# Layer norm averages in one matmul: sums folded to 64 partitions, and attention issued three steps sooner

## The chip, the core and the metric

One NeuronCore of a Trainium2 chip runs the kernel. The metric is the device time of one execution in microseconds; for the kernel before, three runs gave a median of 1599.13 us. TensorE is called PE here, VectorE DVE, ScalarE ACT, GpSimd POOL and SyncE SP, as in the profile.

## The reference

A block with layer norm ahead of each half, on x of shape (2, 4096, 256), in fp32:

```
def _layernorm(x, axis=-1, eps=1e-05):
    m = jnp.mean(x, axis=axis, keepdims=True)
    v = jnp.var(x, axis=axis, keepdims=True)
    return (x - m) / jnp.sqrt(v + eps)
...
x = x + attn(_layernorm(x))     # mixes of x and the token before; k, v, r; a scan over time (WKV); W_o
x = x + ffn(_layernorm(x))      # silu(w1 h) * (w2 h), gelu(h1 .), gelu(h2 .), w3; hidden width 1024
```

Each linear layer of the ffn has weights of -1, 0 and 1 and one scale per output. The attention part is an RWKV time mix: k, v and r are products of mixed inputs with 256 x 256 weights, the WKV recurrence runs along the 4096 tokens, and its result times sigmoid(r) goes through W_o.

## The kernel before

**Layout and tiles.** Features lie on partitions (256 features are two halves of 128), tokens along the free dimension. The tokens are cut into 16 tiles of 512. For each tile the work is: layer norm (`normalise`), attention (`attention`), a second layer norm at attention's end, and `ffn`.

**Precision.** An ffn operand is split into a rounded part hi and a remainder lo (`split`, L190: ACT copies to the rounded type, DVE subtracts), and each weight block is multiplied with both (`split_product`, L180, lines 185 and 186). A product for attention (`product`, L178) is in fp32 and takes two passes in the records, each about twice as long.

**Layer norm.** A mean over 256 features is a sum over partitions, made on PE with the constant matrix `mean_wr` (all entries 1/256), which also spreads the result over all partitions. `layernorm` (L201) adds the two halves into `both` (L206), and `average` (L195) splits that sum into hi and lo and runs two matmuls into one PSUM bank. The centred halves (L212) are squared on ACT (L217), added (L218), averaged in the same way, then root (L220, ACT), reciprocal (L222, DVE) and the multiplication (L224). Tiles 1 to 15 have two such norms each, so two means and two variances. Tile 0 has a function of its own (`first_layernorm`) that the change doesn't touch.

**Order.** The functions are generators. While `ffn(i)` runs, its loop also advances `attention(i+1)` and `normalise(i+2)`. `ffn` has 26 steps: 8 gated products (pa and pb), 8 products of the first hidden layer, 8 of the second (both called ph), and 2 outputs (po). This order of writing is only a start: the framework schedules instructions on each engine when the program is built, so that the built order departs from it, but later steps come later. [...] The loop in the kernel before is:

```
            if step >= NH:
                next(ahead, None)
            if step > 2 * NH - 2 and step % 2:
                next(further, None)
```

Here NH is 8, `ahead` is `attention(i + 1)` and `further` is `normalise(i + 2)`. The pieces of attention are: three mixes (mx, L313 and L314), then for each half h a group of products ps_k, ps_v, ps_r and three pieces of `wkv`, then the output products ps_o with the addition to x (L335), and the three pieces of the second norm, after which x2 is split (x2_hi, x2_lo).

**Buffers.** The products of the ffn rotate through 4 PSUM banks, those of attention through 3, and all averages share 1. Three x tiles rotate; the load of a new one (POOL's queue) waits for the output transfer of the tile that had the buffer. The blocks of h2 come through SP's queue. `compare` (L163) holds copies of weights against the originals, in the same loop[...]. A second program, `general_block`, follows under a condition that isn't met here.

Of the kernel before, what the change touches and what calls it, by code (L numbers as in the profile page):

```python
# [7 lines left out]
F32 = mybir.dt.float32  # L8
F32R = mybir.dt.float32r
AF = mybir.ActivationFunctionType  # L10
ALU = mybir.AluOpType

P = 128
B, T, D, HID = 2, 4096, 256, 1024
TS = 512
ND = D // P
NH = HID // P
# [21 lines left out]
@with_exitstack  # L39
def tile_rwkv_block(  # L40
    ctx: ExitStack,
    tc: tile.TileContext,
    x: bass.AP,
    vecs: bass.AP,
    w_attn: bass.AP,
    w1: bass.AP,
    w2: bass.AP,
    h1: bass.AP,
    h2: bass.AP,
    w3: bass.AP,  # L50
    out: bass.AP,
):
    nc = tc.nc
    flags = ctx.enter_context(tc.tile_pool(name="flags", bufs=1))
    with ExitStack() as inner:
        inexact = split_block(inner, tc, flags, x, vecs, w_attn, w1, w2, h1, h2, w3, out)
    count = nc.values_load(inexact, min_val=0, max_val=1)
    with tc.If(count > 0):
        with ExitStack() as inner:
            general_block(inner, tc, x, vecs, w_attn, w1, w2, h1, h2, w3, out)  # L60


def split_block(ctx, tc, flags, x, vecs, w_attn, w1, w2, h1, h2, w3, out):
# [3 lines left out]
    tensor, vector, scalar = nc.tensor, nc.vector, nc.scalar  # L67
# [4 lines left out]
    one = ctx.enter_context(tc.tile_pool(name="one", bufs=1))  # L72
# [5 lines left out]
    ps_sum = ctx.enter_context(tc.tile_pool(name="ps_sum", bufs=1, space=bass.MemoryType.PSUM))  # L78
# [46 lines left out]
    mean_wr = const.tile([P, P], F32R, name="mean_wr")  # L125
# [29 lines left out]
    pieces = []  # L155
    for sb, src in ((w1_sb, w1), (w2_sb, w2), (h1_sb, h1), (w3_sb, w3)):
        n = src.shape[1] * src.shape[2] // PIECE
        sb, src = (t.rearrange("p a b -> p (a b)") for t in (sb, src))
# [21 lines left out]
    def split_product(psum, weights, src):  # L180

        n = len(src)
        for c in range(n):
            hi, lo = src[c]
            tensor.matmul(psum, weights(c), hi, start=c == 0, stop=False)  # L185
            tensor.matmul(psum, weights(c), lo, start=False, stop=c == n - 1)  # L186

    marks = {}

    def split(hi, lo, full):  # L190

        marks["scalar"] = scalar.activation(hi, full, AF.Copy)  # L192
        marks["split"] = vector.tensor_tensor(lo, full, hi.bitcast(F32), ALU.subtract)  # L193

    def average(psum, both):  # L195

        pieces = one.tile([P, 2, TS], F32R, tag="sums", name="sums")
        split(pieces[:, 0, :], pieces[:, 1, :], both)
        split_product(psum, lambda c: mean_wr, [(pieces[:, 0, :], pieces[:, 1, :])])

    def layernorm(src, new_xc, tag, pause=False):  # L201


        both = one.tile([P, TS], F32, tag=tag, name="both")
        mean = ps_sum.tile([P, TS], F32, tag="ps", name="mean")
        vector.tensor_tensor(both, src[:, 0, :], src[:, 1, :], ALU.add)  # L206
        average(mean, both)
        if pause:
            yield
        xc = new_xc()  # L210
        for h in range(ND):
            vector.tensor_tensor(xc[:, h, :], src[:, h, :], mean, ALU.subtract)  # L212
        yield
        sq = wide.tile([P, ND, TS], F32, tag="wide", name="sq")
        var = ps_sum.tile([P, TS], F32, tag="ps", name="var")
        rstd = one.tile([P, TS], F32, tag=tag, name="rstd")
        scalar.activation(sq, xc, AF.Square)  # L217
        vector.tensor_tensor(sq[:, 0, :], sq[:, 0, :], sq[:, 1, :], ALU.add)  # L218
        average(var, sq[:, 0, :])
        scalar.activation(rstd, var, AF.Sqrt, bias=eps)  # L220
        yield
        vector.reciprocal(rstd, rstd)  # L222
        for h in range(ND):
            vector.tensor_tensor(xc[:, h, :], xc[:, h, :], rstd, ALU.mult)  # L224
        yield
# [58 lines left out]
    def normalise(i):  # L284

        x_sb = loaded.pop(i)
        if i + 1 < len(tiles):
            loaded[i + 1] = load_x(i + 1)
        xn = []

        def new_xn():

            xn.append(one.tile([P, ND, TS + 1], F32, tag="xn", name="xn"))
            if tiles[i][1] == 0:
                vector.memset(xn[0][:, :, 0:1], 0.0)
            else:
                vector.tensor_copy(xn[0][:, :, 0:1], prev)
            return xn[0][:, :, 1:]

        yield from layernorm(x_sb, new_xn, "rstd1", pause=i == 1)  # L300
        vector.tensor_copy(prev, xn[0][:, :, TS:])
        normal[i] = (x_sb, xn[0])

    def attention(i):

        first = tiles[i][1] == 0
        x_sb, xn = normal.pop(i)
        mixed = []
        for m in range(3):
            mx = wide.tile([P, ND, TS], F32, tag="wide", name="mx")  # L310
            for h in range(ND):
                j = m * ND + h
                vector.tensor_scalar(mx[:, h, :], xn[:, h, 0:TS], unmix[:, j : j + 1], None, ALU.mult)  # L313
                vector.scalar_tensor_tensor(  # L314
                    mx[:, h, :], xn[:, h, 1:], vec[:, j : j + 1], mx[:, h, :], ALU.mult, ALU.add
                )
            mixed.append(mx)
            yield

        y = wide.tile([P, ND, TS], F32, tag="wide", name="y")  # L320
        for h in range(ND):
            kvr = []
            for m, name in enumerate("kvr"):
                ps = ps_attn.tile([P, TS], F32, tag="pa", name="ps_" + name)
                product(
                    ps, lambda c: wa_sb[:, m, c, h * P : (h + 1) * P], [mixed[m][:, c, :] for c in range(ND)]
                )
                kvr.append(ps)
            yield
            yield from wkv(h, *kvr, y, first)  # L330

        for h in range(ND):
            ps = ps_attn.tile([P, TS], F32, tag="pa", name="ps_o")
            product(ps, lambda c: wa_sb[:, 3, c, h * P : (h + 1) * P], [y[:, c, :] for c in range(ND)])
            vector.tensor_tensor(x_sb[:, h, :], x_sb[:, h, :], ps, ALU.add)  # L335
        yield
        x2 = wide.tile([P, ND, TS], F32, tag="wide", name="x2")
        yield from layernorm(x_sb, lambda: x2, "rstd2")
        x2_hi = one.tile([P, ND, TS], F32R, tag="x2_hi", name="x2_hi")
        x2_lo = one.tile([P, ND, TS], F32R, tag="x2_lo", name="x2_lo")  # L340
        split(x2_hi, x2_lo, x2)
        got[i] = (x_sb, [(x2_hi[:, c, :], x2_lo[:, c, :]) for c in range(ND)])
# [186 lines left out]
    def run(steps):  # L529
        for _ in steps:  # L530
            pass
# [15 lines left out]
    for i in range(len(tiles)):  # L547
        ahead = attention(i + 1) if i + 1 < len(tiles) else iter(())
        further = normalise(i + 2) if i + 2 < len(tiles) else iter(())
        for step, _ in enumerate(ffn(i, *got.pop(i))):  # L550
            if i == 0 and step % 2:
                next(second, None)

            if step >= NH:
                next(ahead, None)
            if step > 2 * NH - 2 and step % 2:
                next(further, None)
        run(ahead)
        run(further)
# [287 lines left out]
```

## Time and profile before

| | us |
|---|---|
| three runs, median (lowest to highest) | 1599.13 (1598.64 to 1599.64) |
| the profiled execution, own time | 1599.32 |
| its span, first to last instruction | 1597.5 |
| matmuls of the averages, both parts: mean 18.9 + 12.6, variance 12.2 + 12.4 | 56.1 busy, 120 matmuls |
| ACT table loads with Gelu (L508), and with the root (L220) | 130.9 (102 loads), 38.5 (30 loads) |
| reciprocal of the norm, DVE (L222) | 100.4 (30, 3.35 each) |

The span is what the profile covers; the own time has 1.8 us more. In a group's row the numbers behind the bar are the busy time of all its instructions and the mean of one in ns, then the idle time of the engine just ahead of them and what ended it. Matmuls overlap in the records: a hidden-layer matmul lasts 0.39 us there, but the next starts 0.23 us later.

In the steady part a tile takes about 96.5 us (the output products ps_o of two tiles in a row start 96.45 us apart, at 710.23 and 806.67). The last PE instruction ends at 1588.3 us; what follows is the last output transfer and the check of the comparisons.

### The profile page before, as it was taken

The page shows a single profiled execution, that of the slowest core. Times are in us where ns is not written, and L with a number is a line of the kernel's source. Part 1 is how long each engine was busy: PE and PEld are TensorE (multiplying, and loading weights), DVE is VectorE, ACT ScalarE, POOL GpSimd, SP SyncE. Part 2 cuts the span into 40 slices and gives each one's busy share as a digit, 9 for nine tenths or more (in the row PEclk, how much of TensorE's full clock was granted, in tenths as well). Part 3 has the DMA queues.
Part 4 walks back from the last instruction along what each step waited for, and adds up shares of the span by engine and source line. Part 5 has one row for each costly group of instructions (what it writes and reads, how often), then busy time and mean ns, then how long its engine had stood idle before and what let it go on. Part 6 is the DMA issues. An engine that isn't in the chain of part 4 may idle for free.

```text
span 1597.5 us, 16645 instructions
## 1 busy us (share of the span) xinstructions
PE 1576.5 (99%) x6370; PEld 1198.3 (75%) x6370; DVE 1063.3 (67%) x1707; ACT 1005.7 (63%) x1337; POOL 58.0 (4%) x92
## 2 busy tenths in 40 slices
PE   8899999999999999999999999999999999999997
PEld 4677778777777777777777777777778777787786
DVE  5767577685766958668585676857668575675521
ACT  5566666756757567576666657567576666657542
POOL 2000000000000000000000000000000000000000
PEclk9899999999999999999999999999999999999999
DMA  9103122130311203112030221203112031211202
GB/s 357 38 0 109 37 80 73 33 119 14 106 54 53 93 14 119 40 56 96 20 119 27 80 72 46 93 14 106 40 53 86 7 105 40 67 60 33 93 8 74
DMA packets 36790, 109.17 MB, mean 68 GB/s; under 512 B 3680, under 2 KB 12384, under 8 KB 36192
## 3 DMA queue, kind: packets, MB, share of 16 engines
q1 hardware_dynamic: 19552, 68.71, 13.0%
q0 software_dynamic: 16736, 38.80, 7.9%
q8 instruction: 52, 0.85, 0.2%
q10 hardware_dynamic: 416, 0.52, 0.1%
q14 instruction: 34, 0.28, 0.1%
HBM read 99.64 MB, written 12.58 MB: 70 GB/s over the span
## 4 chain that ended last, share of the span: by engine, by line
PE 80%; issue 15%; DMA 1%; ACT 1%; DVE 1%; POOL 0%; SPq 0%; POOLq 0%; ACTq 0%
PE ph L185 24%; PE ph L186 24%; PE pa L185 3%; PE pb L185 3%; PE pa L186 3%; PE pb L186 3%; PE po L186 3%; PE po L185 3%; PE ps_r L178 3%; PE ps_k L178 3%; PE ps_v L178 3%; PE ps_o L178 3%; DMA wa_sb<-in_w_attn 1%; PE mean L185 0%; PE mean L186 0%
## 5 line engine op out<-in xcount | busy, mean ns | idle before, releaser
L185 PE MATMUL ph<-hi,h_sb 128*128 128x512 f32 x2048 | 812.3, 397 | 0.0
L186 PE MATMUL ph<-lo,h_sb 128*128 128x512 f32 x2048 | 799.9, 391 | 0.0
L185 PEld LDWEIGHTS ph<-hi,h_sb 128*128 128x128 f32 x2048 | 384.6, 188 | 89.7 <-issue 7.4
L186 PEld LDWEIGHTS ph<-lo,h_sb 128*128 128x128 f32 x2048 | 384.7, 188 | 87.2 <-issue 7.2
L511 DVE TENSOR_TENSOR lo<-full,hi 128x512 fp32r<-128x512 f32 x256 | 175.1, 684 | 314.8 <-ACT full L510 314.6
L508 ACT ACTIVATE hi<-ph,vec 128x512 fp32r<-128x512 f32 x256 | 176.0, 687 | 288.4 <-PE ph L186 287.0
L510 ACT ACTIVATE full<-ph,vec 128x512 f32<-128x512 f32 x256 | 174.4, 681 | 0.0
L508 ACT ACT_TABLE_LOAD x102 | 130.9, 1283 | 1.8
L492 ACT ACTIVATE gated<-pa,vec 128x512 f32<-128x512 f32 x128 | 86.9, 683 | 63.2 <-PE pa L186 60.2
L493 DVE SCALAR_TENSOR_TENSOR gated<-pb,vec,gated 128x512 f32<-128x512 f32 x128 | 95.3, 748 | 30.1 <-PE pb L186 21.6
L185 PE MATMUL pa<-x_hi,w_sb 128*128 128x512 f32 x256 | 103.9, 406 | 1.7 <-ACT gated L492 1.7
L186 PE MATMUL pa<-x_lo,w_sb 128*128 128x512 f32 x256 | 103.4, 404 | 0.0
L222 DVE RECIPROCAL rstd<-rstd 128x512 f32<-128x512 f32 x30 | 100.4, 3346 | 3.3 <-ACT rstd L220 3.2
L185 PE MATMUL pb<-x_hi,w_sb 128*128 128x512 f32 x256 | 102.0, 398 | 0.0
L186 PE MATMUL pb<-x_lo,w_sb 128*128 128x512 f32 x256 | 100.8, 394 | 0.0
L192 ACT ACTIVATE hi<-gated 128x512 fp32r<-128x512 f32 x128 | 80.3, 629 | 32.2 <-DVE gated L493 30.9
L186 PE MATMUL po<-lo,w_sb 128*128 128x512 f32 x256 | 98.1, 392 | 0.0
L185 PE MATMUL po<-hi,w_sb 128*128 128x512 f32 x256 | 97.9, 391 | 0.0
L193 DVE TENSOR_TENSOR lo<-gated,hi 128x512 fp32r<-128x512 f32 x128 | 87.6, 685 | 12.5 <-ACT hi L192 9.1
L314 DVE SCALAR_TENSOR_TENSOR mx<-xn,vec,mx 128x512 f32<-128x512 f32 x90 | 66.2, 745 | 0.4
L260 ACT ACTIVATE sc<-sc 128x512 f32<-128x512 f32 x32 | 20.3, 633 | 67.0 <-DVE sc L258 66.9
L185 PEld LDWEIGHTS pa<-x_hi,w_sb 128*128 128x128 f32 x256 | 48.5, 189 | 17.2 <-ACT gated L492 4.1
(140 smaller groups left out, 1774.9 us busy)
## 6 DMA issues: line engine op xcount, KB each, us to landing
h_sb<-h_hbm SPq DMA_DIRECT2D x128, 512.0 KB, 3.3
out<-x_sb POOLq DMA_DIRECT2D x16, 512.0 KB, 3.1
raw<-in_h POOLq DMA_DIRECT2D x32, 256.0 KB, 3.1
x_sb<-in_x POOLq DMA_DIRECT2D x14, 512.0 KB, 4.0
h_sb<-in_h POOLq DMA_DIRECT2D x1, 4096.0 KB, 20.2
h_hbm<-in_h POOLq DMA_DIRECT2D x8, 512.0 KB, 25.3
w_sb<-in_w POOLq DMA_DIRECT2D x3, 1024.0 KB, 10.4
raw<-in_w POOLq DMA_DIRECT2D x12, 256.0 KB, 2.8
```

Of the source, the lines that this page charges most:

```text
L178: tensor.matmul(psum, weights(c), src[c], start=c == 0, stop=c == n - 1)
L185: tensor.matmul(psum, weights(c), hi, start=c == 0, stop=False)
L186: tensor.matmul(psum, weights(c), lo, start=False, stop=c == n - 1)
L192: marks["scalar"] = scalar.activation(hi, full, AF.Copy)
L193: marks["split"] = vector.tensor_tensor(lo, full, hi.bitcast(F32), ALU.subtract)
L222: vector.reciprocal(rstd, rstd)
L314: vector.scalar_tensor_tensor(mx[:, h, :], xn[:, h, 1:], vec[:, j : j + 1], mx[:, h, :], ALU.mult, ALU.add)
L492: scalar.activation(full, pa, AF.Silu, scale=col(S1, f))
L493: vector.scalar_tensor_tensor(full, pb, col(S2, f), full, ALU.mult, ALU.mult)
L508: scalar.activation(hi, ps, AF.Gelu, scale=col(scales, f))
L510: scalar.activation(full, ps, AF.Gelu, scale=col(scales, f))
L511: vector.tensor_tensor(lo, full, hi.bitcast(F32), ALU.subtract)
```

## The change

`average` now takes the two addends, makes the sum itself, and folds it: the upper 64 partitions of the sum are copied by ACT to the lower 64, DVE adds the lower 64, and the result (64 partitions) is split so that hi lies on partitions 0 to 63 and lo on 64 to 127 of one tile. One matmul with the same constant matrix then sums both. The squares are no longer added in place but into the tile `both`. And the loop takes four pieces of attention at step 8, and pieces of the norm after next at steps 12, 14, 16 and 18 instead of 15, 17, 19 and 21.

```
-    def average(psum, both):
-
-        pieces = one.tile([P, 2, TS], F32R, tag="sums", name="sums")
-        split(pieces[:, 0, :], pieces[:, 1, :], both)
-        split_product(psum, lambda c: mean_wr, [(pieces[:, 0, :], pieces[:, 1, :])])
+    def average(a, b, tag, name):
+
+
+        both = one.tile([P, TS], F32, tag=tag, name="both")
+        vector.tensor_tensor(both, a, b, ALU.add)
+        folded = one.tile([P // 2, TS], F32, tag="folded", name="folded")
+        marks["scalar"] = scalar.activation(folded, both[P // 2 :, :], AF.Copy)
+        vector.tensor_tensor(folded, folded, both[: P // 2, :], ALU.add)
+        parts = one.tile([P, TS], F32R, tag="parts", name="parts")
+        split(parts[: P // 2, :], parts[P // 2 :, :], folded)
+        psum = ps_sum.tile([P, TS], F32, tag="ps", name=name)
+        tensor.matmul(psum, mean_wr, parts, start=True, stop=True)
+        return psum
...
-        both = one.tile([P, TS], F32, tag=tag, name="both")
-        mean = ps_sum.tile([P, TS], F32, tag="ps", name="mean")
-        vector.tensor_tensor(both, src[:, 0, :], src[:, 1, :], ALU.add)
-        average(mean, both)
+        mean = average(src[:, 0, :], src[:, 1, :], tag, "mean")
...
-        var = ps_sum.tile([P, TS], F32, tag="ps", name="var")
+        scalar.activation(sq, xc, AF.Square)
+        var = average(sq[:, 0, :], sq[:, 1, :], tag, "var")
         rstd = one.tile([P, TS], F32, tag=tag, name="rstd")
-        scalar.activation(sq, xc, AF.Square)
-        vector.tensor_tensor(sq[:, 0, :], sq[:, 0, :], sq[:, 1, :], ALU.add)
-        average(var, sq[:, 0, :])
...
-            if step >= NH:
+            for _ in range(0 if step < NH else 4 if step == NH else 1):
                 next(ahead, None)
-            if step > 2 * NH - 2 and step % 2:
+            if step > 2 * NH - 6 and step % 2 == 0:
                 next(further, None)
```

## The prediction

> **What bounds the kernel now.** I read the busy shares first, then the list of waits (PE's alone), the chain, and the timeline of one tile.
>
> ```profile
> PE 1576.5 (99%) x6370; PEld 1198.3 (75%) x6370; DVE 1063.3 (67%) x1707; ACT 1005.7 (63%) x1337; POOL 58.0 (4%) x92
> PE 80%; issue 15%; DMA 1%; ACT 1%; DVE 1%; POOL 0%; SPq 0%; POOLq 0%; ACTq 0%
> PE pa L185 <- ACT gated L492: 1.7, 2, 1.3
> ```
>
> PE is busy for the whole span, and the chain of work that ended last lies on it. The third line is the only wait of PE listed after the first tile's attention ends (some 57 us); the others add to under 11 us, all earlier. So the span is a count of matmuls times their spacing, and ACT and DVE (about a third idle) count only where PE would wait for them. In the stage table of one tile (the gated products, hidden layer 1, hidden layer 2, the output product) only the first presses on DVE, 13.46 of 15.40 us:
>
> ```profile
> 736.50:751.90 15.40, 15.40 (x66) 12.12 (x65) 13.46 (x22) 9.84 (x16) 1.43 (x2) 1.00 0.20 70
> 751.90:793.00 41.10, 41.10 (x162) 30.12 (x161) 22.27 (x42) 25.40 (x34) 1.10 (x2) 1.00 0.04 13
> 793.00:829.00 36.00, 36.00 (x152) 27.94 (x151) 27.98 (x41) 26.39 (x34) 1.51 (x2) 1.00 0.36 117
> ```
>
> (Columns: length; busy us and count of PE, weight loads, DVE, ACT, POOL; granted clock.) The clock is full throughout, so no gain can come from it.
>
> **What is removed.** PE's timeline around the mean of an attention output:
>
> ```profile
> 719.42 0.39 PE L185 MATMUL ph<-hi,h_sb 128*128 128x512 f32 x1
> 719.66 0.50 PE L185 MATMUL mean<-sums,mean_wr 128*128 128x512 f32 x1
> 720.00 0.39 PE L186 MATMUL ph<-lo,h_sb 128*128 128x512 f32 x1
> 720.22 0.39 PE L185 MATMUL ph<-hi,h_sb 128*128 128x512 f32 x1
> 720.45 0.44 PE L186 MATMUL mean<-sums,mean_wr 128*128 128x512 f32 x1
> 720.72 0.39 PE L186 MATMUL ph<-lo,h_sb 128*128 128x512 f32 x1
> ```
>
> The durations overlap; the price is the distance between starts: 0.22 to 0.23 us for a hidden matmul, 0.34 and 0.27 for these two. Variance matmuls take 0.24 (708.67 to 708.91), and a mean behind the attention products 0.23 (694.82 to 695.05). I take 0.235. [...] 15 tiles x 2 norms x 2 averages = 60 matmuls x 0.235 = 14.1 us[...]. The built order of the changed program has exactly 60 matmuls fewer on PE, so this is real whatever else happens.
>
> **What is added.** Each average gets an ACT copy (partitions 64 to 127 down to 0) and a DVE add on 64 partitions. The variance's old add in place becomes the add into "both", at no difference. No row shows an instruction on 64 partitions. Nearest are the same operations at full height:
>
> ```profile
> L192 ACT ACTIVATE sums<-both 128x512 fp32r<-128x512 f32 x30 | 18.9, 629 | 16.9 <-DVE both L206 16.4 <-DVE prev L301 0.5
> L193 DVE TENSOR_TENSOR sums<-both,sums 128x512 fp32r<-128x512 f32 x30 | 20.7, 689 | 3.0 <-ACT sums L192 1.9
> ```
>
> Bounds: half of it if height counted, twice if crossing partitions took two passes. [...] I take the rows: 0.63 and 0.69. That is 60 x 0.63 = 38 us more on ACT and 60 x 0.69 = 41 on DVE, or 65% and 69% busy. It hides beside PE unless an average's operand comes late, and each now comes about 1.4 us later (0.63 + 0.69 + hand-overs). The operands of the parts (split) keep their price. Three table loads more (1.28 us each, in the first tile's part of ACT's order) hide too or appear below.
>
> **What moves.** Steps count from 0: 8 gated, 8 of layer 1, 8 of layer 2, 2 outputs. The loop now takes four pieces of attention(i+1) at step 8, and starts normalise(i+2) at step 12 instead of 15. In the built order of a middle tile, the first k, v, r group stands behind one layer-1 product instead of four, the second behind five instead of eight. normalise issues an x load through POOL's queue; but that load waits for a buffer freed by the output transfer, so its order on POOL is unchanged, and SP's queue (the h blocks) is untouched. Where cover goes:
>
> 1. Layers 1 to 2. Before, the second k, v, r group (12 passes x 0.43) and a mean pair stood between the last layer-1 product and the first of layer 2, 5.6 us. Now nothing does: the first layer-2 product needs the last hi after 14 matmuls (3.2 us), the lo after 15 (3.4). Queued on ACT: Gelu hi, Gelu full (starts 0.6 apart, 0.68 long), then DVE's subtraction 0.69, 2.0 with hand-overs. ACT is also behind by table loads and the square of xn (1.06); following the order with the trace's durations, ACT reaches this Gelu 0.5 to 0.7 us after the product. 2.7 of 3.4: cost nothing, 0.7 spare. Without that cover each late us counts 14 times.
> 2. The mean of an attention output. It stands 9 matmuls into the third product after ps_o, 2 x 3.64 + 2.05 = 9.3 us after it. ACT must first do the Gelu hi of the second product (ends 7.3 + 0.2 + 0.6), then the parts copy 0.63, then DVE 0.69: 9.4. Margin about -0.1.
> 3. Its variance stands 11 matmuls into the fifth: 17.3 us. Likewise 14.8 + 0.2 + 0.6 + 0.63 + DVE's queue and 0.69: 17.0 to 17.3. Margin 0 to 0.3.
> 4. The variance of xn stands between the two ps_o products, 0.7 spare. Its mean was split 41 us before use (652.8 against 694.2), so that is safe.
> 5. The gated stage. The sum of x waits for the x load on DVE, with gated results queued behind it:
>
> ```profile
> 746.52 0.69 DVE L206 TENSOR_TENSOR both<-x_sb 128x512 f32<-128x512 f32 x1 [0.50 <-DMA x_sb<-in_x]
> 747.13 0.75 DVE L493 SCALAR_TENSOR_TENSOR gated<-pb,vec,gated 128x512 f32<-128x512 f32 x1
> ```
>
> It lands 10.0 us after the stage's start; the same order stands in the changed program. The gated result of f = 4 frees the bank that pb of f = 6 needs at 12.1 (6.5 pairs x 1.86); it would be ready at 11.5. Spare 0.6. The mixes of the next tile now stand before this stage, which takes 2.3 us off DVE here (0.87 + 1.41, at 737.84) where the added DVE fold puts 0.69 back.
>
> Points 2 and 3 are the tight ones; before, the same places stood 0.1 to 0.25 us behind their operands and PE did not wait. I charge 0.07 us per middle tile, 14 x 0.07 = 1.0 us.
>
> **First tile.** Before the first ps_v PE waits for scaled weights until 23.97 anyway, so the longer mean of tile 1 costs nothing there. In the first gated stage the order has the root, then the reciprocal (3.35 us) of tile 1's norm, later than before, in front of the gated results. Followed with the trace's durations, the stage ends at 76.05 instead of 75.36: 0.7. The four attention pieces at step 8 then need six mixes (2 x 3 x 1.1 us of DVE) that had been spread over later steps: the third mix is some 0.6 late. Together +1.3.
>
> **Sum.** 1599.3 (the profiled execution; span 1597.5 and 1.8 around it; 0.2 above the median, which I neglect) - 14.1 + 1.0 + 1.3 = 1587.5.
>
> **Rivals.**
> - A, as summed, 1585 to 1590: 0.64. For it: idle thirds on ACT and DVE, points 1, 4, 5 with spare.
> - B, the longer chains are late at points 2 and 3 by 0.2 to 0.4 us each: 14 x 2 x 0.3 = 8.4 back, about 1595 (1591 to 1599). For it: margins near zero, and one Gelu out of place is 0.7. Against: PE never waited at such places before. 0.20. Most of this lies below 1596.
> - C, slower: an instruction that crosses from partitions 64 up to 0 takes twice its row. Then copy, add and the lo half add 0.63 + 0.69 + 0.69 = 2.0 us to each of the four averages of a tile; where three of four have 0 to 0.7 spare, about 1.5 x 3 x 14 = 63, about 1650. It decides from 0.3 us per average (14 / 42) beyond the spare. Nothing in the trace shows such a crossing[...]. 0.07.
> - D, the change does not do what it says: PE's order is fixed when built and has 60 fewer, but if a removed matmul only filled a gap in which PE waited for a weight load, PE would keep the gap and the time would be 1599. Against: spacings around the pair add up. 0.04.
> - E, better: removed matmuls cost 0.3 as at 719.66 and the first tile costs nothing: 1599.3 - 18 = 1581. 0.05.
>
> A run tells 0.2%, 3.2 us, from no change: faster is below 1596, slower above 1602. Faster: A, E and 0.16 of B, 0.85; same: 0.03 of B and D, 0.07; slower: C and the last 0.01 of B, 0.08. The range leaves out C, D and half of E and goes to the upper end of B's bulk: 1584 to 1595.
>
> **What would show it.** PE matmuls 6310; a middle tile's period 96.5 less 0.94 plus 0.07, 95.6 us; the 64-partition rows near 0.63 and 0.69; for A, PE's waits after 77 us sum to under 3 us. Waits of PE's mean and var rows for DVE parts mean B or C (the row's length tells which); a wait of the first layer-2 product for lo means point 1 failed; a first stage ending before 75.5 or after 77 means the first-tile term is wrong.

## The result and the profile after

| | before | after |
|---|---|---|
| median of six runs each (lowest to highest), us | 1598.89 (1597.3 to 1599.78) | 1585.3 (1583.61 to 1586.25) |
| profiled execution, own time (span), us | 1599.32 (1597.5) | 1583.61 (1581.8) |
| one middle tile, output products to output products, us | 96.44 | 95.63 |

The ratio of after to before is 0.9915, with a 95% interval of 0.9902 to 0.9928: 0.85% faster. The forecast of 1587.5 is 2.2 us above it, and the time lies in the range. The profiled execution of after is the lowest of its six, so the two traces are 15.7 us apart where the medians are 13.6 apart; the accounts below are of the traces. In one of the six executions of a later run, the one with only attention moved, the granted clock was 0.751 and the time 1956.68 us; its ratio leaves that execution out.

The busy shares and the chain of work that ended last, as the page of after has them:

```profile
PE 1560.2 (99%) x6310; PEld 1183.7 (75%) x6310; DVE 1102.5 (70%) x1767; ACT 1043.3 (66%) x1400; POOL 58.6 (4%) x92
...
PE 79%; issue 15%; DVE 2%; ACT 2%; DMA 1%; POOL 0%; SPq 0%; POOLq 0%; DVEq 0%; ACTq 0%
```

PE has 60 matmuls fewer (6370 to 6310) and is still busy for 99% of a shorter span. DVE has 60 instructions more and ACT 63 (60 copies, 3 table loads); neither bounds the kernel. The stage table of the same tile as before (gated products, layer 1, layer 2, output product; columns as before):

```profile
727.20:742.10 14.90, 14.90 (x65) 12.03 (x64) 11.22 (x17) 9.77 (x16) 1.43 (x2) 1.00 0.21 71
742.10:782.00 39.90, 39.90 (x155) 28.82 (x155) 25.91 (x49) 30.25 (x38) 1.10 (x2) 1.00 0.05 14
782.00:815.50 33.50, 33.50 (x140) 25.95 (x139) 29.09 (x41) 22.47 (x31) 1.51 (x2) 1.00 0.31 103
```

PE fills every stage. The gated stage has lost DVE work (13.46 to 11.22 us), since the mixes now stand before it; the hidden layers took on what was added. The boundaries are not quite at the same instructions as before, so the lengths are not to be subtracted stage by stage.

The rows of the fold and of the parts, among the groups of after:

```profile
L193 DVE TENSOR_TENSOR parts<-folded,parts 64x512 fp32r<-64x512 f32 x60 | 41.1, 685 | 28.4 <-ACT parts L192 27.3
L202 DVE TENSOR_TENSOR folded<-folded,both 64x512 f32<-64x512 f32 x60 | 40.6, 677 | 2.0 <-ACT folded L201 2.0
L201 ACT ACTIVATE folded<-both 64x512 f32<-64x512 f32 x60 | 37.9, 631 | 13.3 <-DVE both L199 12.1
L192 ACT ACTIVATE parts<-folded 64x512 fp32r<-64x512 f32 x60 | 37.4, 623 | 12.0 <-DVE folded L202 12.0
```

On half as many partitions ACT's copy took 631 ns and DVE's add 677, where the nearest rows on all 128 had 629 and 689 before. ACT's copy from partitions 64 to 127 down to 0 to 63 took 631 ns, the one that stays in place (L192) 623. So the fold adds 631 + 677 ns and two hand-overs to the way from the sum to the matmul.

PE's timeline at the mean of an attention output, which before stood as a pair:

```profile
1085.23 0.39 PE L186 MATMUL ph<-lo,h_sb 128*128 128x512 f32 x1
1085.46 0.39 PE L185 MATMUL ph<-hi,h_sb 128*128 128x512 f32 x1
1085.82 0.50 PE L206 MATMUL mean<-parts,mean_wr 128*128 128x512 f32 x1
1086.16 0.39 PE L186 MATMUL ph<-lo,h_sb 128*128 128x512 f32 x1
1086.39 0.39 PE L185 MATMUL ph<-hi,h_sb 128*128 128x512 f32 x1
```

DVE's timeline of the two instructions that make its operand:

```profile
1082.95 0.68 DVE L202 TENSOR_TENSOR folded<-folded,both 64x512 f32<-64x512 f32 x1
1085.08 0.69 DVE L193 TENSOR_TENSOR parts<-folded,parts 64x512 fp32r<-64x512 f32 x1 [1.45 <-ACT parts L192]
```

One matmul is left of two. It starts 0.36 us after its neighbour instead of 0.23, because its operand is done at 1085.08 + 0.69 = 1085.77. The matmul after it follows 0.34 later instead of 0.23. In between DVE stood idle for 1.45 us: ACT makes the hi part of a fold that was ready at 1083.63 only at 1084.43, behind a Gelu. These short waits are not in the list of waits. That list (PE's, its first three lines) shows only the first tile, and after 77 us no more than 0.6 us in all:

```profile
PE var L372 <- DVE sq L368: 3.0, 3, 1.6
PE mean L206 <- DVE parts L193: 2.0, 1, 2.0
PE pa L185 <- ACT gated L495: 1.4, 2, 1.1
```

The mean in it is the one at 18.8 us, ahead of the first tile's products. A wait of 0.1 us must be read from the distance between starts: of the 28 averages of the middle tiles that follow a hidden product, 18 start late (more than 0.237 us after it).

**Where the 15.7 us came from**, by the starts of each tile's first gated product in the two traces: 4.0 before the first (56.57 to 52.53); tile 0 about nothing (it is 0.1 longer, with five matmuls removed); tiles 1 to 13 give 13 x 0.865 = 11.2; the rest some 0.4.

### The profile page after: what moved, and what is told of

Its sections match the earlier page's. It is cut to its first block, busy times and chain, and to the rows that moved or that the text cites. A ratio compares the mean times of both kernels' runs of the same rounds, so it can differ in the third digit from the quotient of the medians.

```text
span 1581.8 us, 16635 instructions
## 1 busy us (share of the span) xinstructions
PE 1560.2 (99%) x6310; PEld 1183.7 (75%) x6310; DVE 1102.5 (70%) x1767; ACT 1043.3 (66%) x1400; POOL 58.6 (4%) x92
## 4 chain that ended last, share of the span: by engine, by line
PE 79%; issue 15%; DVE 2%; ACT 2%; DMA 1%; POOL 0%; SPq 0%; POOLq 0%; DVEq 0%; ACTq 0%
PE ph L186 24%; PE ph L185 24%; PE pa L185 3%; PE pb L185 3%; PE pb L186 3%; PE pa L186 3%; PE po L186 3%; PE po L185 3%; PE ps_k L178 3%; PE ps_o L178 3%; PE ps_r L178 3%; PE ps_v L178 3%; DMA wa_sb<-in_w_attn 1%; PE mean L206 1%; PE var L206 0%
## 5 line engine op out<-in xcount | busy, mean ns | idle before, releaser
L496 DVE SCALAR_TENSOR_TENSOR gated<-pb,vec,gated 128x512 f32<-128x512 f32 x128 | 95.6, 748 | 55.8 <-PE pb L186 30.1
L192 ACT ACTIVATE hi<-gated 128x512 fp32r<-128x512 f32 x128 | 80.5, 630 | 25.5 <-DVE gated L496 23.9
L259 DVE TENSOR_TENSOR_SCAN lm<-vec,lm,ps_k 128x512 f32<-128x512 f32 x32 | 40.9, 1278 | 46.8 <-PE ps_k L178 45.3
```

Of the source, the lines that this page charges most:

```text
L496: vector.scalar_tensor_tensor(full, pb, col(S2, f), full, ALU.mult, ALU.mult)
```

## The experiments

The theory, P in the expectations, is that of the prediction: the gain is 60 matmuls of PE's time, less short waits at the averages of the second norm; the moved steps give nothing themselves and are cover for the longer way to each average. Its rivals: that the move of the loop is what gains, that the fold alone would do, and that the work at the start makes the difference. Kernels are described against after, if not said otherwise. Ratios are to the kernel before, with 95% intervals; it took 1598.4 to 1598.7 beside these runs.

### The two halves of the change

**Fold alone** (loop as before):

```
-            for _ in range(0 if step < NH else 4 if step == NH else 1):
+            if step >= NH:
                 next(ahead, None)
-            if step > 2 * NH - 6 and step % 2 == 0:
+            if step > 2 * NH - 2 and step % 2:
                 next(further, None)
```

> The change's average with the loop of before. Theory P (time follows the count of PE's matmuls, the earlier placement only gives the longer chain its cover): the 60 matmuls go (-14), but in the built order the variance of the second norm now stands 9 matmuls into the first output product, with 23 matmuls (5.3 us) and the next k and v groups (3.4 us) ahead of the gated stage, and root with its table load, reciprocal, two multiplications and the split behind it take 8 to 9 us: 0 to 1 us of wait per tile, so 1586 to 1598, about 1591. Rival Q (the gain is that of the earlier placement): about 1599. Rival N (placement does not matter): 1585, as the changed kernel.

Measured: 1615.15, ratio 1.0101 (1.0085 to 1.0116): slower than before. The forecast missed by 24 us. PE's list of waits, of which the first two lines were 1.7 us in all before:

```profile
PE pa L185 <- ACT gated L495: 9.8, 8, 1.6
PE ph L185 <- ACT gated L495: 9.0, 6, 1.6
PE var L206 <- DVE parts L193: 3.3, 7, 0.5
```

The waits are mostly of the gated stage, not of the averages. DVE's timeline ahead of one such stage, the next tile's:

```profile
834.13 3.34 DVE L225 RECIPROCAL rstd<-rstd 128x512 f32<-128x512 f32 x1
837.39 0.65 DVE L526 SCALAR_TENSOR_TENSOR x_sb<-po,vec,x_sb 128x512 f32<-128x512 f32 x1
837.96 1.28 DVE L227 TENSOR_TENSOR x<-x,rstd 128x512 f32<-128x512 f32 x2
```

ACT's, where the normalised x gets its hi part:

```profile
839.27 1.06 ACT L192 ACTIVATE x_hi<-x 128x1024 fp32r<-128x1024 f32 x1 [6.27 <-DVE x L227]
```

And PE's first gated product:

```profile
840.52 0.80 PE L185 MATMUL pa<-x_hi,w_sb 128*128 128x512 f32 x1
```

The variance now came so late, in the output products, that the reciprocal (3.34 us) ran when the next tile was already due. ACT waited 6.27 us for the normalised x, and PE took up the tile 0.2 us after its hi part. The stage that follows takes 19.74 us to the first layer-1 product, where the same tile of before took 15.8. Most of the 3.9 is work that was moved there: eight passes of the next attention's k and r products (0.43 us each), where before has two; some 1.4 are left for waits (an estimate). Tiles alternate: one takes 99.73 us with 42 such passes, the next 96.35 with 22, where 32 are the share of each.

The long waits are in the second kind of tile. There the steps that belong to those products fall into the gated stage, and ACT changes its table of functions between them and the Silu: five to seven table loads (1.28 us each) in that stage, in the middle tiles of after one at most. ACT's timeline in the tile that starts at 1035.64:

```profile
1049.67 1.28 ACT L495 ACT_TABLE_LOAD   x1
1050.97 1.27 ACT L495 ACTIVATE gated<-pa,vec 128x512 f32<-128x512 f32 x2
```

And PE's:

```profile
1051.71 0.50 PE L185 MATMUL pa<-x_hi,w_sb 128*128 128x512 f32 x1 [1.56 <-ACT gated L495]
```

No run took the table loads away, so that they make the waits is read from the trace.

**Move alone** (the loop of after, the averages of before):

> The average of before with the loop of the change. P: no matmul goes, PE had no waits after the first tile for a placement to remove: 1597 to 1601, the first tile up to 1.3 us worse. Q: 1585 to 1590.

Measured: 1599.17, ratio 1.0002 (0.9994 to 1.0011), a middle tile 96.39. As P has it: the move alone gives nothing. It is not the source of the gain, and the fold alone is a loss; together they gain 13.6.

**Each half of the move with the fold.** First the next attention is moved, the norm is not:

```
-            if step > 2 * NH - 6 and step % 2 == 0:
+            if step > 2 * NH - 2 and step % 2:
                 next(further, None)
```

> The changed kernel with the next-but-one norm at its old steps (15, 17, 19, 21); only attention is three steps sooner. P: the cover that the fold needs is that of the second norm at attention's end, so all of it stays: 1584 to 1587. If the earlier next-but-one norm is the cover: towards the 1615 of the fold without the move.

Measured: 1592.1, ratio 0.9961 (0.9949 to 0.9974), a middle tile 96.11. Missed by 5 us. PE's timeline at a variance:

```profile
900.85 0.39 PE L185 MATMUL ph<-hi,h_sb 128*128 128x512 f32 x1
901.34 0.50 PE L206 MATMUL var<-parts,mean_wr 128*128 128x512 f32 x1
901.68 0.39 PE L186 MATMUL ph<-lo,h_sb 128*128 128x512 f32 x1
```

0.49 before it and 0.34 after it, instead of 0.23 each. With the norm at its old steps the averages of the two norms follow each other, on ACT and DVE too, and three of four per tile wait. Then the norm moved, the attention not:

```
-            for _ in range(0 if step < NH else 4 if step == NH else 1):
+            if step >= NH:
                 next(ahead, None)
```

> The change's average, with attention at its old steps and only the next-but-one norm at 12, 14, 16, 18. P: the second norm still ends too late for the next tile's gated stage, as in the fold without a move (1615): 1605 to 1618. If the earlier next-but-one norm alone gives the cover: 1585 to 1592.

Measured: 1597.07, ratio 0.999 (0.9982 to 0.9999), a middle tile 96.45. Missed again, in the other direction: I had put all of the cover down to the attention. In its list of waits the gated ones of the fold alone are gone, and the first is

```profile
PE var L206 <- DVE parts L193: 5.0, 13, 0.4
```

thirteen waits, one per tile. So each half of the move covers another thing:

| | averages of before | folded averages |
|---|---|---|
| loop of before | 1598.9 | 1615.15 |
| norm moved | | 1597.07 |
| attention moved | | 1592.1 |
| both moved | 1599.17 | 1585.3 |

### What a removed matmul is worth

The kernel before, with the averages' lo product left out (they are then averages of rounded sums):

```
-        split_product(psum, lambda c: mean_wr, [(pieces[:, 0, :], pieces[:, 1, :])])
+        tensor.matmul(psum, mean_wr, pieces[:, 0, :], start=True, stop=True)
```

> Before, with the lo part of each sum left out of its product (the split is still made; the averages are those of rounded sums). 60 matmuls go and no chain grows. P: 60 x 0.235 = 14.1 less, 1584 to 1586; if a removed matmul is worth 0.30, 1581; if PE keeps a gap in its place, 1597 or more. The distance to the changed kernel is what the fold's longer chains cost: P says 1 to 3 us in the changed kernel's disfavour.

Measured: 1579.24, ratio 0.9876 (0.9861 to 0.9891); a middle tile goes from 96.44 to 95.33. It missed by 5: 3.7 us of that are at the start (below), and the four matmuls of a tile are worth 1.10, 0.28 each, not 0.235. Of its 41 averages behind a hidden product only two start late, and the usual interval is 0.23. In before, the mean pair cost 0.34 and 0.27 (at 719.66 and 720.45): part of what was removed was not a matmul but the slow step after a wait.

### The length of the way to an average

**Longer.** ACT's fold copy is made twice:

```
+        scalar.activation(folded, both[P // 2 :, :], AF.Copy)
         marks["scalar"] = scalar.activation(folded, both[P // 2 :, :], AF.Copy)
```

> The change with ACT's fold copy made twice, so each chain is 0.63 us longer and ACT has 38 us more. P: the builder puts the averages later, PE waits 0.1 to 0.3 us more at two of four averages: 1 to 5 us above the changed kernel, 1586 to 1590. Rival C (the chains set the time, PE waits out every addition at the two tight averages): 14 x 2 x 0.63 = 18 above, about 1603.

Measured: 1587.97, ratio 0.9927 (0.9914 to 0.9941), a middle tile 95.80, 0.17 more than after. Four copies of 0.63 more in each tile cost PE 0.17: ACT's added work is nearly all covered, but not quite. The built order differs too, so this is not the price of the copy alone: the variance of xn stands two passes later among the output products of attention, and the two averages of the second norm stand six and four matmuls sooner behind them.

**Shorter.** The hi part is made by DVE, which made the fold just before, so that two hand-overs and ACT's queue drop out:

```
-        split(parts[: P // 2, :], parts[P // 2 :, :], folded)
+        vector.tensor_copy(parts[: P // 2, :], folded)
+        marks["split"] = vector.tensor_tensor(
+            parts[P // 2 :, :], folded, parts[: P // 2, :].bitcast(F32), ALU.subtract
+        )
```

> The changed kernel with the rounded part (hi) of the folded sum made by a DVE copy instead of ACT, so that one of the chain's two turns in ACT's queue goes. In the changed kernel a tile spends 0.30 us on PE's waits at the second norm's two averages (0.14 + 0.12 + 0.06). Theory L (the chain's length sets these waits): they go, 14 x 0.3 = 4 less, about 1581. Theory J (the builder places each average where it expects its operand, whatever the length, and is off by a tenth of a microsecond): 1584 to 1587.

Measured: 1582.0, ratio 0.9893 (0.9879 to 0.9908). Its runs (1580.12 to 1582.38) all lie below those of after. A middle tile has 95.35, 0.28 less. PE's timeline at a mean:

```profile
797.23 0.39 PE L185 MATMUL ph<-hi,h_sb 128*128 128x512 f32 x1
797.46 0.40 PE L209 MATMUL mean<-parts,mean_wr 128*128 128x512 f32 x1
797.69 0.39 PE L186 MATMUL ph<-lo,h_sb 128*128 128x512 f32 x1
```

The new copy among the groups:

```profile
L204 DVE CAST parts<-folded 64x512 fp32r<-64x512 f32 x60 | 25.6, 427 | 1.0
```

0.23 before and after the mean: the wait is gone, and with it the slow step behind it (0.34 in after). Three of the 28 averages behind hidden products still start late, where after had 18. This is the loss that was left in after, 0.3 us a tile; this version beats both kernels.

**DVE for both steps.** The fold copy goes to DVE as well:

```
-        marks["scalar"] = scalar.activation(folded, both[P // 2 :, :], AF.Copy)
+        vector.tensor_copy(folded, both[P // 2 :, :])
```

> The changed kernel with both ACT steps of the average, the fold copy and the rounded part, made by DVE copies. L: the chain leaves ACT's queue entirely, the waits at the second norm's averages are gone (they fell from 0.30 to about 0.03 us a tile when one step left), so little more is to be had there, and DVE, 70% busy, gets some 25 us more: 1580 to 1583. If DVE becomes the late one in the gated stage: above 1585.

Measured: 1590.91, ratio 0.9951 (0.9938 to 0.9965). Missed by 8. The mean of the second norm waits again (0.51 before it), and a middle tile has 95.73; the gated stages of the middle tiles have no wait in PE's list. That DVE's fuller queue is the cause is likely, but no run shows it. Early in the run PE waits for a weight block:

```profile
129.98 0.47 PE L185 MATMUL ph<-hi,h_sb 128*128 128x512 f32 x1 [2.83 <-DMA h_sb<-h_hbm]
```

That block was issued on SP's queue at 125.8 us, 4 us later than in after. Why is open; no run was made on it. It matters as much as the mean: tile 0 has 104.42 us, 4.6 more than with the hi part alone on DVE. The shortest way on paper is not the best: of the two steps taken from ACT, only the one that stood behind a Gelu in ACT's queue was worth it.

### The start

**Tile 1's attention later.** In the first tile the four pieces at step 8 are one again:

```
-            for _ in range(0 if step < NH else 4 if step == NH else 1):
+            for _ in range(0 if step < NH else 4 if step == NH and i else 1):
```

> The changed kernel with attention of tile 1 at one piece per step, as before; all later tiles as changed. The prediction charged 0.6 us to the six mixes of tile 1 that come together; the trace shows some 1.3 us of losses in the first tile. P: 0.5 to 1.3 less, 1584 to 1585. If the first tile's losses come from the reciprocal in the gated stage alone: no difference.

Measured: 1585.02, ratio 0.9916 (0.9903 to 0.9928), not to be told from after. In its trace the first gated stage is 1.0 us longer, with a granted clock of half speed from 67 to 70 us that after lacks, and the rest of tile 0 is 0.34 shorter. So the bunched mixes seem to cost 0.3, where I had charged 0.6; what the stage would have been at full clock is not seen.

**Idle matmuls ahead of the first output products**, in the kernel before:

```
+        spare = ps_ffn.tile([P, TS], F32, tag="pf", name="spare")
+        with tc.issue_after(marks["product"].ins):
+            for _ in range(10):
+                tensor.matmul(
+                    spare.rearrange("p (a b) -> p a b", b=P), mean_wr, mean_wr.unsqueeze(1).to_broadcast([P, TS // P, P]),
+                    start=True, stop=True,
+                )
```

> Before, with ten idle matmuls of 0.23 us put into PE's wait ahead of the first tile's output products (37.9 to 40.6 us). In the trace of before the granted clock is half from 41.4 to 44.8, and these products take 5.2 us instead of 3.6. Clock theory: the wait lets the clock fall; with it filled the products take 3.6 us and the time is 1.7 less, about 1597. If the half clock comes at its own time whatever PE does: no difference.

Measured: 1597.27, ratio 0.9991 (0.9983 to 0.9999). The first output products (ps_o, 16 of them) in the stage tables of before and of this kernel, each with the stretch ahead of it; the granted clock is the third column from the end. Before:

```profile
36.90:40.65 3.75, 1.05 (x3) 0.19 (x2) 3.71 (x8) 2.35 (x4) 0.00 (x0) 1.00 1.59 396
40.65:45.90 5.25, 5.25 (x17) 4.33 (x18) 1.87 (x5) 0.00 (x0) 0.00 (x0) 0.67 0.59 229
```

The kernel with idle matmuls:

```profile
37.40:41.10 3.70, 3.30 (x14) 2.06 (x12) 3.67 (x8) 2.29 (x4) 0.00 (x0) 1.00 1.57 389
41.10:44.65 3.55, 3.55 (x16) 3.14 (x17) 1.87 (x5) 0.00 (x0) 0.00 (x0) 1.00 0.75 303
```

In before PE pauses 2.7 us for DVE's y and then runs at a granted clock of 0.67: 5.25 us. With the pause filled the same work takes 3.55 at full clock. The half clock after the pause is thus worth 1.7, and the kernel as a whole became 1.45 faster. In after the pause is 0.9, the clock stays full, and ps_o takes 3.83: 1.4 of the start's 4 us. PE's first output products in before:

```profile
40.65 5.41 PE L452 MATMUL ps_o<-y,wa_sb 128*128 128x256 f32 x16 [2.70 <-DVE y L279]
```

in after:

```profile
38.58 4.00 PE L455 MATMUL ps_o<-y,wa_sb 128*128 128x256 f32 x16 [0.90 <-DVE y L282]
```

and DVE's work that they wait for, in before:

```profile
39.91 1.34 DVE L279 TENSOR_TENSOR y<-so,ps_r 128x512 f32<-128x512 f32 x3
```

and in after:

```profile
37.85 0.68 DVE L282 TENSOR_TENSOR y<-so,ps_r 128x512 f32<-128x512 f32 x1
...
39.68 0.75 DVE L282 TENSOR_TENSOR y<-so,ps_r 128x256 f32<-128x256 f32 x2 [0.55 <-DVE so L280]
```

When the program was built anew, the first half's y was put ahead of the other half's last steps on DVE. ps_o starts 2.1 us sooner; 0.3 of it is an earlier landing of weights. In every trace here whose averages are folded or have no lo part, ps_o starts at 38.3 to 40.0 and takes 3.7 to 4.0; in before and with the move alone it starts at 40.4 to 40.7 and takes 5.4. So this gain hangs on the averages and not on the move, but it comes by way of the builder's order. No run changed that order alone.

**Idle matmuls before the first variance**, added to the version with DVE's hi part:

```
-            keep_warm(4)
+            keep_warm(10)
```

> The changed kernel with the rounded part on DVE, and ten instead of four idle matmuls in the first tile's wait for the variance (2.3 us instead of 0.9 of a wait of some 2.9), after which traces show the granted clock at half for 3.4 or 6.8 us. Clock theory: without that half clock the first ffn products start 0.7 to 2 us sooner: 1580 to 1581.5. If the wait is filled but the half clock comes anyway, from the next waits (0.9 us each): 1582.

Measured: 1581.73, ratio 0.9892 (0.9877 to 0.9907), not to be told from the 1582.0 without it. Its stretch of half clock near 50 us is gone, but another stands at 63.9 to 67.3.

## Why the prediction was right, step by step

- **60 matmuls x 0.235 = 14.1.** The count is right, the price too low: 0.28 each where the pair carried slow steps after waits, as the run without the lo part shows. That is about 0.16 more per tile. The reading of single rows (0.34 and 0.27 at the mean, 0.23 elsewhere) had it; I took the low ones for all.
- **1.0 us for waits at points 2 and 3.** The places are right, the size is not: 0.07 per tile was charged, and 0.30 is there. The mean waits 0.14 and its successor starts 0.115 late; the variance has 0.06. The step that failed is the margin counted as wait only: behind the waiting mean stood a slow step too (0.34 to the next start instead of 0.23). The two errors cancel nearly, by luck: 95.63 for the tile, where 95.6 was forecast. The sign named for rival A, less than 3 us of waits after 77 us, came (0.6 in the list) and says nothing of these 4 us.
- **Point 1, layers 1 to 2.** Confirmed to a tenth. The lo of the first layer's last block is done at 1071.12 + 0.69 = 1071.81 and used at 1072.46: 0.65 spare, 0.7 forecast.
- **Point 4, the variance of xn between the ps_o products.** PE does not wait, but the spare is 0.16 (operand 1073.84, matmul 1074.00) and not 0.7.
- **Point 5, the gated stage.** No wait of PE in the middle tiles. DVE's wait for the x load is rarer: three of 0.2 to 0.7 us after the first tile, where before had five.
- **The added operations.** 0.63 and 0.69 were taken from rows at full height, 0.631 and 0.677 measured on 64 partitions, the first of them with the crossing. Rival C, whose 0.07 was the author's estimate, is out. DVE 70% and ACT 66%, where 69% and 65% were forecast.
- **The first tile, +1.3.** Five matmuls fewer (1.2 us at 0.235), and it is 0.1 longer: 1.3 of loss, as forecast. But the sign that was named against this term came: the first gated stage ends at 71.10, which is 75.14 with the start's 4.0 put back, and so before 75.5. Its length (18.79 to 18.57 us) can't be compared bare, since 1.9 us of it ran at half clock in before and 0.75 in after. Without that help the first tile's loss would be some 1.8 (an estimate that takes half the time at half clock as lost), so the term was too small. The waits that it spoke of are there: in this stage of before three products start 1.74, 0.46 and 0.72 us after the one ahead of them, in after 1.53, 1.18 and 0.68, together 0.5 more, where 0.7 was forecast.
- **What I did not have at all** is the start: 4.0 us before the first gated product. I had compared the orders around the averages and along the steps of the first ffn, not DVE's order in the first attention, which holds PE up for 2.7 us in the trace of before. "The clock is full throughout, so no gain can come from it" was read from a middle tile; in the first 60 us of before it is half from 10.7 to 17.5, from 41.4 to 44.8 and from 51.7 to 58.5, and 1.4 of the 4.0 came from it. With the rest the sum stands, in part because errors cancel: 14.1 - 1.0 - 1.3 = 11.8 forecast, 15.7 - 4.0 = 11.7 in the traces.
- **The medians show 2 us less than the traces.** The clock of the executions that were traced is part of this. Of the executions of before that ran beside the experiments, the nine with a mean granted clock of 0.992 took 1599.8 us on average, the twelve with 0.995 or more 1598.0. Before was traced at 0.993 (1599.32 us), after at 0.996, in the lowest of its six; with tile 1's attention later, the trace has 0.994 and 1585.23 us. The rest is open.

Rival B had the right place, and half of its 8.4 us is there (14 x 0.3 = 4.2); the price of the pair, set too low, hid it. Rival E's price of 0.3 for a removed matmul was near the measured 0.28; its first tile without loss was not.

## What to carry to other kernels

PE was full here (99% busy), and what was added off PE was free only where PE's operand still came in time; look at every place where the longer way ends, and at what takes its old cover, for the fold without the move costs 1% and with it gains 0.85%. Read short waits from the distance between starts, before and behind the waiting matmul: the list of waits does not show 0.1 us, and fourteen tiles multiply it. After any edit compare the built order of the start too, where a pause of PE was paid twice in before, as time (2.7 us) and as clock (1.7).

## What the runs showed of the hardware

- **Behind an average that started late, the next matmul was late too.** A mean of after that starts 0.25 us after its neighbour, some 20 ns late (at 133.14), is followed 0.34 us later instead of 0.23. Intervals before, at and behind the mean at 1085.82 in after: 0.23, 0.36, 0.34; with the wait removed, at 797.46 with DVE's hi part: 0.23, 0.23, 0.23. So such a wait cost some 0.11 us beyond itself. Seven variances of the middle tiles of after that start on time are followed late as well, after 0.25 to 0.30; why is open.
- **Two pauses of PE were followed by half clock.** After the 2.7 us pause in before, the records show half speed from 41.4 to 44.8. With DVE doing both steps of the average, the stretch after the 2.83 us wait, and the one behind it:

```profile
130.00:133.90 3.90, 3.90 (x10) 3.07 (x11) 1.83 (x4) 0.00 (x0) 0.00 (x0) 0.56 0.37 146
134.00:137.00 3.00, 3.00 (x15) 2.46 (x14) 2.41 (x5) 1.25 (x2) 0.00 (x0) 1.00 0.06 14
```

10 matmuls in 3.9 us at a clock of 0.56, then 15 in 3.0 at 1.00. Ten idle matmuls in the pause of before took the stretch at 41 away: the output products took 3.55 us at a clock of 1.00 instead of 5.25 at 0.67. The stretch at 41 and the one behind the 2.83 us wait last 3.4 us, though others last 6.8 (51.66 to 58.49 in before), and the changes of clock in before (10.70, 17.53, 41.42, 44.83, 51.66, 58.49) lie multiples of 3.41 us apart. That every such pause costs this is not shown, as the place and number of such stretches in the first 70 us differ from kernel to kernel.
- **Height did not count in these rows.** 64 partitions took ACT 623 to 631 ns and DVE 677 to 685, 128 took 629 and 689; DVE's copy with rounding of 64x512 took 427 ns, a third less than ACT's 623.
